# A cap of 768 KB on the transfers under way from SyncE's queue during the second pass

## The chip, the cores and the metric

The kernel runs on one core of one Trainium2 chip. The metric is the device time of one execution in microseconds. Before the change it is 1311.23 us, the median of three runs (1306.88 to 1315.88).

## The reference: what is computed

There are 32 batches (graphs) of 512 nodes with 128 features each, `x[32, 512, 128]`, and a symmetric 0/1 adjacency matrix with ones on its diagonal per batch, `adj[32, 512, 512]`, all in fp32. Four layers follow one another; each takes `h = relu(layernorm(x))` and adds its result to `x`:

```
layer 0  q, k, v = relu(h Wq' + bq), relu(h Wk' + bk), relu(h Wv' + bv)
         x += softmax_j(where(adj, q k', -9e15)) v
layer 1  dyn = conv3(h[:, last 128 nodes]);  lw = lstm(dyn)      # 128 steps, hidden size 128
         x += sigmoid((D^-1/2 (adj + I) D^-1/2 h) lw)
layer 2  four graph layers: tanh(cat(src_agg, own, dst_agg) Wu + bu),
         with adj normalised by rows and by columns; the 3rd and 4th also take earlier ones
x       += layer 2
layer 3  x += prelu(adj (h W'))
```

The LSTM runs over 128 time steps for all 32 batches at once. It needs the last 128 nodes of every batch after layer 0, and nothing of the other nodes. Everything from the sigmoid of layer 1 on needs `lw`, and so the end of the LSTM.

## The kernel before

`symmetric` records every operation in a planner (`Plan.op`) with the engines that may run it, an estimated duration, a rank, what it reads and writes, and a gap in which its result is on the way. `Plan.run` then simulates five engines with these estimates, gives every operation an engine and a start, sorts all of them by start, and emits them in that order. So each engine's queue, SyncE's (SP's) among them, is a fixed order of instructions; an instruction that waits holds back all that stands behind it on the same engine. A DMA is recorded by the helper `DMA` (line 853) with its size in KB; its place on SP's engine takes `0.1 + kb / 315` us in the plan, and its landing a gap of 2.0 us or, in the second pass, `LANDED = 3.8` us. Nothing of the plan's times is in the program; only the order is. What runs before what is kept by semaphores.

The work is in three passes over the batches and the LSTM.

- First pass, `pass_1` (ranks from 10,000): the layer norm, keys, values and the last 128 nodes of layer 0. Keys and hidden vectors (`f_dkq`), values (`f_dv`) and the last 128 rows (`f_dl`) go to HBM.
- The LSTM (`lstm`, ranks below 1,000 and 2,000 on): per step 16 small matmuls into `f_z` (L1224), two ScalarE tanh (L1250, L1262), VectorE (L1256, L1257), a tanh (L1264), VectorE (L1268, and L1269 for the transpose into `f_seq`), and then the next step.
- Second pass, `pass_2` (ranks 20,000 to 20,279 for batches 0 to 27; the last four batches have ranks above 30,000): layer 0 for the first 384 nodes. It is planned into the gaps of the LSTM. Per batch, SP's queue loads `f_h` (L1289) and `f_k` (L1290) from `f_dkq`, four blocks of the adjacency matrix of 256 KB each, `f_a` (L1293; L1298 with 192 KB for batches 22 to 25 and 28 to 31), the values `f_v` (L1300), `f_x` (L1301) and, for the batches that do the sums of layer 1 here, `f_dl` (L1304). ScalarE squares `f_a` into `f_ar` (L1363), TensorE makes the scores `f_s` (L1315), ScalarE their exponentials (L1318), VectorE multiplies with the mask (L1319), TensorE adds up `f_po` (L1324), VectorE updates `f_x` (L1328, L1330). For batches 0 to 21 the aggregation of layer 1, `f_pg` (L1409), follows. SP stores `f_dx` (L1335) and `f_dgT` (L1351). After four of the batches a `fold` of layer 2's weights is planned, with loads `f_rowb` (L986) and `f_w` (L988) of 384 to 768 KB.
- The rest, `rest` (L1423 on): for one batch after another all that needs `lw`, ended by the store to `out` (L1574). The first two turns (batches 26 and 27) have their ranks moved back by 9,950, so that they also lie between 20,000 and 30,000.

SP's queue carries 914 transfers; 88 of them are transposing transfers, which are recorded directly and not by `DMA`. The framework gives SP's DMAs eight semaphores in turn, and a DMA waits for the one eight before it, so that at most eight transfers are under way.

Of the kernel before, what the change touches and what calls it, by code (L numbers as in the profile page):

```python
# [492 lines left out]
class Cell:  # L493


    def __init__(self, pool, tag, shape, dtype, name, whole=False, filled=False):
        self.pool, self.tag, self.shape, self.dtype, self.name = pool, tag, shape, dtype, name
        self.whole, self.filled = whole, filled
        self.size = 1
        for n in (shape or ())[1:]:  # L500
            self.size *= n
        self.place = None
        self.ahead = 0
        self.marked = True
        self.real = None
        self.left = 0
        self.free_at = 0.0
        self.parts = {}
# [7 lines left out]


class Op:
    __slots__ = ("engines", "rank", "no", "deps", "cells", "waits", "ready", "end", "engine", "start", "next", "gap", "tiled", "patience")


class Plan:
# [22 lines left out]
    def __init__(self, bufs, fifo, banks):  # L545
        self.banks = banks
        self.last = float("inf")
        self.soon = 0.0
        self.spared = float("inf")
        self.left = 0  # L550
        self.sealed = 0
        self.kept = ("mm", "gs",)
        self.ops = []
        self.bufs = bufs
        self.made = {}
        self.fifo = {t: [] for t in fifo}
# [12 lines left out]
    def op(self, engines, rank, reads=(), writes=(), after=(), gap=0.0, tiled=False):  # L569

        o = Op()
        o.engines, o.rank, o.no, o.gap = engines, rank, len(self.ops), gap
        o.tiled = tiled
        o.patience = 0.15
        deps = set(after)
        cells = []
        for acc, is_write in [(a, False) for a in reads] + [(a, True) for a in writes]:
            c, part = acc if isinstance(acc, tuple) else (acc, None)
            if c not in cells:
                cells.append(c)  # L580
            for key, (ws, rs) in c.parts.items():
                if part is None or key is None or key == part:
                    deps.update(ws)
                    if is_write:
                        deps.update(rs)
            mine = c.parts.setdefault(part, ([], []))
            if is_write:
                c.parts[part] = ([o], [])
            else:
                mine[1].append(o)  # L590
        deps.discard(o)
        o.deps = list(deps)
        o.cells = [c for c in cells if c.pool is not None]
        for c in o.cells:
            c.left += 1
        self.ops.append(o)
        return o

    def run(self, tc, queues):
        import bisect  # L600
# [14 lines left out]
        for o in ops:  # L615
            if o.rank >= self.last:
                k, sub = divmod(o.rank - self.last, 10)
# [49 lines left out]
        def room(o):  # L667

            at = 0.0
            need = {}  # L670
            ahead = 0
            for c in o.cells:
                if c not in seen:
                    ahead = max(ahead, c.ahead)
                    if c.tag in self.fifo and self.fifo[c.tag][turn[c.tag] + need.get(c.tag, 0)] is not c:
                        return None
                    need[c.tag] = need.get(c.tag, 0) + 1
            for t, n in need.items():
                spare = n + ahead + (t == self.banks and o.rank >= self.spared and self.left > 0)
                if len(slots[t]) < spare or len(slots[t]) == spare and t in self.kept and by_rank and o.rank > by_rank[-1].rank + 12:  # L680
                    return None
                at = max(at, sorted(slots[t])[n - 1])
            return at
# [5 lines left out]
        tiled = False  # L689
        by_rank = sorted((o for o in ops if o.rank >= 10_000 and o not in apart), key=lambda o: -o.rank)  # L690
        while done < len(ops):
            best = None
            for e, cands in pools.items():
                first = None
                held = expected.get(e)
                for rank, no, o in cands:
                    r = room(o)
# [22 lines left out]
            s, e, o = best  # L720
# [6 lines left out]
            if e == "PE":  # L727
                tiled = o.tiled
# [22 lines left out]
            done += 1  # L751
        self.order = order
        order.sort(key=lambda o: (o.start, o.no))
        with tc.manual_schedule(engines=queues):
            for o in order:
                o.engines[o.engine][1]()


def symmetric(ctx, tc, x, adj, weights, cols, rows, lstm_b, prelu_a, out, fail):
# [26 lines left out]
    SOON = 9_950.0  # L786
# [18 lines left out]
    plan = Plan(BUFS, ("ar", "x", "inv", "n0", "n1", "n2", "n3", "a"), "mm")  # L805
# [32 lines left out]
    def t_dma(kb):  # L838
        return 0.1 + kb / 315.0
# [11 lines left out]
        return plan.op({"POOL": (t, fn)}, rank, r, w, **k)  # L851

    def DMA(rank, kb, fn, r=(), w=(), **k):
        return plan.op({"SP": (max(0.45, t_dma(kb)), fn)}, rank, r, w, gap=k.pop("gap", 2.0), **k)

    def turn_tiles(dst, src):

# [37 lines left out]
    w = const.tile([P, W_SD[0] + 1, P], FP, name="f_w")  # L895
# [16 lines left out]
    def load(rank, kb, dst, src):  # L912
        c = plan.fixed(dst)
        DMA(rank, kb, lambda: nc.sync.dma_start(dst, src), [], [c])
        return c

    w_att = load(HEAD + 0.1, 192, w[:, :W_CONV, :], weights[:, :W_CONV, :])
    w_cols = load(HEAD + 0.2, 5, colb, cols)
    DMA(HEAD + 0.3, 64, lambda: nc.sync.dma_start(brow[:, BR_V, :], rows[R_V].partition_broadcast(P)), [], [(biases, BR_V)])
    w_conv = load(HEAD + 12, 192, w[:, W_CONV:W_IH, :], weights[:, W_CONV:W_IH, :])  # L920
    w_crow = load(HEAD + 12, 64, conv_row, rows[R_CONV].partition_broadcast(P))
    w_lb = plan.fixed(lb)
    for j in range(P // TURN):
        part = bass.ts(j, TURN)
        DMA(HEAD + 100, 4, lambda part=part: nc.sync.dma_start(
            lb[part], lstm_b.rearrange("s q f -> (s q) f")[:, part].partition_broadcast(TURN)), [], [(w_lb, j)])
# [440 lines left out]
    def diagonal(rank, ar, op):  # L1367
        def fn():
            blocks = flat(ar.t).rearrange("p (k c) -> p k c", c=P)[:, :: NT + 1, :]
            nc.vector.tensor_tensor(blocks, f32(blocks), ident.unsqueeze(1).to_broadcast([P, NT, P]), op)  # L1370
        DVE(rank, t_dve(N), fn, [], [ar])
# [238 lines left out]
    end = lstm()  # L1610
# [5 lines left out]
        rest(b, k, end)  # L1616
    counted()
    E = mybir.EngineType
    plan.last, plan.spared, plan.soon = 30_000, 20_000, SOON
    plan.run(tc, {E.PE, E.Activation, E.DVE, E.Pool, E.SP})  # L1620
    return flag[0]

# [2 lines left out]
@with_exitstack  # L1625
def kernel(
    ctx: ExitStack,
    tc: tile.TileContext,
    x: bass.AP,
    adj: bass.AP,  # L1630
    weights: bass.AP,
    cols: bass.AP,
    rows: bass.AP,
    lstm_b: bass.AP,
    prelu_a: bass.AP,
    out: bass.AP,
):
    nc = tc.nc
    tensors = (x, adj, weights, cols, rows, lstm_b, prelu_a, out)
    flags = ctx.enter_context(tc.tile_pool(name="flags", bufs=1))  # L1640
    fail = flags.tile([P, 1], mybir.dt.int32, name="fail")
    with ExitStack() as pools:
        failed = symmetric(pools, tc, *tensors, fail)
    with tc.If(failed > 0, preferred_fallthrough_block=False), ExitStack() as pools:
        general(pools, tc, *tensors)
# [58 lines left out]
```

## Time and profile before

| | |
|---|---|
| median of three runs | 1311.23 us |
| the profiled execution's own time | 1314.59 us |
| its span in the profile | 1312.7 us |
| TensorE (PE) busy | 1272.8 us, 97% |
| VectorE busy | 988.7 us, 75% |
| ScalarE busy | 834.8 us, 64% |
| GpSimd busy | 393.3 us, 30% |
| DMA moved | 232.82 MB, mean 177 GB/s |
| granted TensorE clock | 0.994 |

The page has one profiled execution. A busy TensorE isn't TensorE at its peak, since matmuls are pipelined and their ends are modelled. The 40 slices of the page are 32.8 us each; the first pass fills slices 1 to 5 and, with the LSTM's first step at 184 us and its last at 500 us, the second pass fills slices 6 to 15. DMA digits are the mean busy share of the core's 16 DMA engines. A landing is the last update of a DMA's semaphore before the semaphore is used again.

### The profile page before, as it was taken

The numbers are of one execution on the slowest core, as the hardware profiler recorded it, in microseconds if no ns is written. First come the engines' busy times: TensorE is split into PE (matmuls) and PEld (weight loads), VectorE is DVE, ScalarE is ACT, GpSimd is POOL, SyncE is SP. The second block draws the span as 40 slices with busy tenths as digits, with TensorE's granted clock in tenths as the row PEclk, the third lists the DMA queues.
The fourth block names the chain that finished last, engine by engine and source line by source line (L and its number), as shares of the span: only waits on it lengthen the run. The fifth ranks groups of instructions, "written<-read, shape, count | busy, mean of one in ns | idle before, by whom it ended". The sixth has DMA issues, their size and how long they took to land.

```text
span 1312.7 us, 32944 instructions
## 1 busy us (share of the span) xinstructions
PE 1272.8 (97%) x12097; PEld 979.3 (75%) x12097; DVE 988.7 (75%) x3274; ACT 834.8 (64%) x2093; POOL 393.3 (30%) x733
## 2 busy tenths in 40 slices
PE   9999999999899999899999999999999999999996
PEld 6888866666567777677878778787787877877774
DVE  7999878778779887677667677676776787787654
ACT  5666667667678654577466666666666666675433
POOL 5655532112213233432213213132131332332000
PEclk9999999999899999999999999999999999999999
DMA  8888888847757867899377776777766465773311
GB/s 264 271 279 271 277 275 252 263 155 240 233 149 251 265 187 168 201 201 218 93 150 163 159 165 152 151 164 160 161 153 143 91 137 139 142 169 65 53 28 36
DMA packets 301259, 232.82 MB, mean 177 GB/s; under 512 B 139680, under 2 KB 246688, under 8 KB 301088
## 3 DMA queue, kind: packets, MB, share of 16 engines
q1 hardware_dynamic: 284192, 213.84, 59.4%
q0 software_dynamic: 16896, 16.78, 8.2%
q8 instruction: 98, 1.61, 0.5%
q14 instruction: 73, 0.60, 0.2%
HBM read 136.98 MB, written 62.13 MB: 152 GB/s over the span
## 4 chain that ended last, share of the span: by engine, by line
PE 85%; DVE 5%; ACT 3%; POOL 2%; DMA 2%; issue 2%; SPq 0%; ACTq 0%; DVEq 0%; POOLq 0%
PE f_pa L1409 17%; PE f_pa L1524 14%; PE f_py L1513 14%; PE f_pg L1409 9%; PE f_po L1324 5%; PE f_s L1315 5%; PE f_z L1224 4%; PE f_p L1565 2%; PE f_pol L1174 2%; PE f_pk L1131 2%; PE f_pv L1147 2%; PE f_pl L1467 2%; PE f_sl L1164 2%; PE f_pd L1199 1%; PE f_pq L1306 1%
## 5 line engine op out<-in xcount | busy, mean ns | idle before, releaser
L1409 PE MATMUL f_pa<-f_ar,f_y 128*128 128x512 f32 x1024 | 295.0, 426 | 2.1 <-ACT f_y L1392 2.1
L1409 PEld LDWEIGHTS f_pa<-f_ar,f_y 128*128 128x128 f32 x1024 | 189.3, 188 | 72.3 <-issue 35.8
L1513 PE MATMUL f_py<-f_wf,f_n 128*128 128x128 f32 x1280 | 173.5, 275 | 0.0
L1513 PEld LDWEIGHTS f_py<-f_wf,f_n 128*128 128x128 f32 x1280 | 164.4, 192 | 10.0 <-issue 1.9
L1524 PE MATMUL f_pa<-f_n,f_wf 128*128 128x512 f32 x320 | 152.9, 593 | 0.1
L1528 ACT ACTIVATE f_n<-f_pa,f_bcol 128x512 f32<-128x512 f32 x128 | 88.2, 689 | 93.6 <-PE f_pa L1524 93.4
L1363 ACT ACTIVATE f_ar<-f_a 128x512 fp32r<-128x512 f32 x216 | 133.7, 622 | 7.1 <-DMA f_a<-in_adj_dram 3.7
L1392 ACT CAST f_y<-f_py 128x512 fp32r<-128x512 f32 x128 | 74.8, 585 | 93.8 <-PE f_py L1513 90.7
L1481 POOL DMA_DIRECT2D f_das<-f_ar x32 | 27.9, 873 | 341.5 <-ACT f_ar L1363 267.9
L1324 PE MATMUL f_po<-f_v,f_e 128*32 128x129 f32 x3072 | 107.0, 274 | 7.5 <-issue 7.4
L1520 DVE TENSOR_TENSOR f_pa<-f_pa,f_inv 128x512 f32<-128x512 f32 x128 | 86.8, 694 | 27.7 <-PE f_pa L1409 27.4
L1324 PEld LDWEIGHTS f_po<-f_v,f_e 128*32 128x32 f32 x3072 | 90.4, 110 | 21.8 <-issue 15.2
L1393 DVE TENSOR_TENSOR f_y<-f_py,f_y 128x512 fp32r<-128x512 f32 x128 | 87.6, 685 | 24.1 <-ACT f_y L1392 23.8
L1315 PE MATMUL f_s<-f_q,f_k 128*32 128x384 f32 x1024 | 103.3, 490 | 0.6 <-issue 0.6
L1224 PE MATMUL f_z<-f_w,f_seq 128*32 128x128 f32 x2040 | 85.1, 277 | 8.6 <-DVE f_seq L1269 4.3
L1524 PEld LDWEIGHTS f_pa<-f_n,f_wf 128*128 128x128 f32 x320 | 57.5, 190 | 47.1 <-issue 37.8
L1224 PEld LDWEIGHTS f_z<-f_w,f_seq 128*32 128x32 f32 x2040 | 54.5, 109 | 45.1 <-ACT f_e L1318 8.7
L1486 DVE SCALAR_TENSOR_TENSOR f_junk<-f_a,f_aT 128x1024 bf16<-128x1024 f32 x64 | 78.1, 1220 | 5.7 <-DMA f_aT<-f_das 4.7
L1409 PE MATMUL f_pg<-f_ar,f_xp_d 128*128 128x512 f32 x256 | 75.2, 417 | 0.5 <-DVE f_lw L870 0.3
L1058 ACT ACTIVATE f_xn_c<-f_x,f_sh_c,f_rs_c 128x128 f32<-128x128 f32 x138 | 58.0, 486 | 24.2 <-DVE f_sh_c L1066 24.1
L1318 ACT ACTIVATE f_e<-f_s 128x384 f32<-128x384 f32 x128 | 60.7, 485 | 19.8 <-PE f_s L1315 14.8
L1513 PE MATMUL f_py<-f_wf,f_T_c 128*128 128x128 f32 x448 | 72.9, 275 | 0.0
(202 smaller groups left out, 2734.9 us busy)
## 6 DMA issues: line engine op xcount, KB each, us to landing
f_a<-in_adj_dram SPq DMA_DIRECT2D x30, 1024.0 KB
f_a<-in_adj_dram SPq DMA_DIRECT2D x96, 256.0 KB
f_das<-f_ar POOLq DMA_DIRECT2D x32, 512.0 KB, 4.8
f_dkq<-f_kh SPq DMA_DIRECT2D x32, 448.0 KB
f_dv<-f_v SPq DMA_DIRECT2D x32, 258.0 KB
f_v<-f_dv SPq DMA_DIRECT2D x32, 258.0 KB
f_x<-in_x_dram SPq DMA_DIRECT2D x32, 256.0 KB
f_al<-in_adj_dram SPq DMA_DIRECT2D x32, 256.0 KB
```

The lines of the kernel that those rows point to most:

```text
L1224: nc.tensor.matmul(z.t[part, k, :, :], h, w[:, m : m + 4, part], start=False, stop=True, skip_group_check=True)
L1315: PE(R, t_mm(NR), lambda s=s, j=j: quarters(lambda p: nc.tensor.matmul(s.t[p], keys.t[:, j * P + p.start : j * P + p.stop], q.t, start=Tru ...
L1324: PE(R, t_mm(P), lambda t=t, j=j: quarters(lambda p: nc.tensor.matmul(po.t[p, t, :], es[j].t[:, t * P + p.start : t * P + p.stop], v.t[:, ...
L1363: ACT(rank, 0.62, lambda t=t: nc.scalar.activation(ar.t[:, t, :], a.t[:, t, :], AF.Square, accum_out=deg.t[:, t : t + 1]), [(a, t)], [(ar, ...
L1392: ACT(rank, t_act(N), lambda: nc.scalar.copy(parts.t[:, :, 0, :], src.t), [src], [(parts, 0)])
L1393: DVE(rank, t_dve(N), lambda: nc.vector.tensor_sub(parts.t[:, :, 1, :], src.t, f32(parts.t[:, :, 0, :])), [src, (parts, 0)], [(parts, 1)])
L1409: nc.tensor.matmul(pg.t, parts.t[:, j, k, :], ar.t[:, j, :], start=(k == 0 and j == 0), stop=(k == 1 and j == NT - 1))
L1486: nc.vector.scalar_tensor_tensor(junk, flat(a.t[:, 2 * k : 2 * k + 2, :]), 1.0, flat(aT.t[:, 2 * k : 2 * k + 2, :]), OP.mult, OP.not_equal ...
L1513: nc.tensor.matmul(py.t[:, j, :], nodes[n].t[:, bass.ts(j, P)], wf[:, W_F[i] + c, 0, :], start=False, stop=(c == nch - 1), skip_group_chec ...
L1520: before = DVE(R, t_dve(N), lambda pa=pa: nc.vector.tensor_mul(pa.t, pa.t, inv_row.t), [inv_row], [pa])
L1524: nc.tensor.matmul(pa.t, wf[:, W_F[i] + c, 1, :], nodes[n].t, start=False, stop=(c == nch - 1), skip_group_check=True)
L1528: ACT(R, 0.57, lambda pa=pa, n=n, i=i: nc.scalar.activation(n.t, pa.t, AF.Tanh, bias=bcol[:, i : i + 1]), [pa], [n])
```

## The change

Every recorded transfer of SP's queue keeps its size in `kb` (0 for the transposing ones). While the instructions are emitted, a list `flight` of all SP transfers in order is kept. After each one `hold_back` is called. If the transfer's rank lies in 20,000 to 30,000 (the second pass of batches 0 to 27, its stores, the folds, and the first two turns of the rest), it goes back through the list, its own size first, until the sum is over 768 KB; on the transfer at which this happens it puts a dependence: this transfer is issued once that one has landed. Other transfers get no dependence, but count. The order of instructions on every engine stays as it was, since the plan doesn't look at `kb`.

```diff
+    def hold_back(self, tc, flight, o):
+
+        if not self.spared <= o.rank < self.last:
+            return
+        kb = 0
+        for ins, more in reversed(flight):
+            if kb + more > self.in_flight:
+                tc.add_manual_dep(flight[-1][0], ins.name, mybir.DependencyInfo(
+                    mybir.DependencyClass.Sync, mybir.DependencyReason.DATA), reason="transfers under way")
+                return
+            kb += more
...
+        flight = []
         with tc.manual_schedule(engines=queues):
             for o in order:
-                o.engines[o.engine][1]()
+                made = o.engines[o.engine][1]()
+                if o.engine == "SP":
+                    flight.append((made.ins, o.kb))
+                    self.hold_back(tc, flight, o)
...
     def DMA(rank, kb, fn, r=(), w=(), **k):
-        return plan.op({"SP": (max(0.45, t_dma(kb)), fn)}, rank, r, w, gap=k.pop("gap", 2.0), **k)
+        o = plan.op({"SP": (max(0.45, t_dma(kb)), fn)}, rank, r, w, gap=k.pop("gap", 2.0), **k)
+        o.kb = kb
+        return o
...
-    plan.last, plan.spared, plan.soon = 30_000, 20_000, SOON
+    plan.last, plan.spared, plan.soon, plan.in_flight = 30_000, 20_000, SOON, 768
```

More of the change, by code (lines that the diff above doesn't have):

```diff
@@ L518 @@
 class Op:
-    __slots__ = ("engines", "rank", "no", "deps", "cells", "waits", "ready", "end", "engine", "start", "next", "gap", "tiled", "patience")
+    __slots__ = ("engines", "rank", "no", "deps", "cells", "waits", "ready", "end", "engine", "start", "next", "gap", "tiled", "patience", "kb")
 class Plan:
@@ L548, in __init__ @@
         self.soon = 0.0
+        self.in_flight = float("inf")
         self.spared = float("inf")
@@ L574, in op @@
         o.patience = 0.15
+        o.kb = 0
         deps = set(after)
```

## The prediction

> **What bounds the kernel now.** I read the page's busy rows first, then the same rows of the second pass alone, then who waits there, then SP's own queue.
>
> ```profile
> span 1312.7 us, 32944 instructions
> PE 1272.8 (97%) x12097; PEld 979.3 (75%) x12097; DVE 988.7 (75%) x3274; ACT 834.8 (64%) x2093; POOL 393.3 (30%) x733
> DMA  8888888847757867899377776777766465773311
> GB/s 264 271 279 271 277 275 252 263 155 240 233 149 251 265 187 168 201 201 218 93 150 163 159 165 152 151 164 160 161 153 143 91 137 139 142 169 65 53 28 36
> ```
>
> TensorE is the busiest engine from end to end, but the change touches the part in which DMA is nearly full: in the first eight slices the rings are eight tenths busy and move 252 to 279 GB/s. The DMA answer for 160 to 480 us, the second pass beside the LSTM, in 40 slices of 8 us, shows what is asked of the queue there:
>
> ```profile
> GB/s 274 271 280 289 278 232 276 234 289 290 257 173 289 62 118 205 253 286 189 275 201 324 93 258 264 242 152 160 74 168 278 264 280 164 274 312 291 234 181 255
> DMA packets 54877, 74.30 MB, mean 232 GB/s; under 512 B 5261, under 2 KB 31469, under 8 KB 54809
> ```
>
> A mean of 232 GB/s made of bursts of 260 to 320 and troughs under 100. The waits of ScalarE in the same stretch show who sets the pace beside DMA:
>
> ```profile
> ACT f_th L1250 <- PE f_z L1224: 48.1, 76, 4.1
> ACT f_tcn L1264 <- DVE f_th L1257: 19.6, 40, 1.2
> ACT f_e L1318 <- PE f_s L1315: 11.3, 8, 4.9
> ```
>
> The LSTM's tanh waits for its own matmuls, 76 times. These stand in TensorE's queue among the matmuls of the second pass, so TensorE's order ties the two together: a second-pass matmul that waits for data holds the LSTM step behind it. No wait for `f_a` is in this list; the loads are in time, though not by much. SP's timeline shows how close the queue runs:
>
> ```profile
> 234.84 0.33 SPq L1335 DMA_DIRECT2D f_dx<-f_x  x1
> 235.21 0.43 SPq L1293 DMA_DIRECT2D f_a<-in_adj_dram  x1
> 235.74 0.39 SPq L1300 DMA_DIRECT2D f_v<-f_dv  x1
> 236.17 0.43 SPq L1301 DMA_DIRECT2D f_x<-in_x_dram  x1
> 236.65 0.49 SPq L1304 DMA_DIRECT2D f_x<-f_dl  x1
> 237.24 0.91 SPq L1289 DMA_DIRECT2D f_h<-f_dkq  x1
> 238.19 0.43 SPq L1290 DMA_DIRECT2D f_k<-f_dkq  x1
> 238.72 1.82 SPq L1293 DMA_DIRECT2D f_a<-in_adj_dram  x4
> 240.83 0.33 SPq L1300 DMA_DIRECT2D f_v<-f_dv  x1
> 241.20 0.43 SPq L1301 DMA_DIRECT2D f_x<-in_x_dram  x1
> 246.43 0.33 SPq L1335 DMA_DIRECT2D f_dx<-f_x  x1
> ```
>
> Thirteen transfers leave within 7 us, one each 0.5 us, far faster than they land: by the landing semaphores `f_a` of 239.61 lands at 245.67. The queue is filled ahead, and that depth keeps the rings busy while SP waits afterwards (241.6 to 246.4).
>
> **What the Trainium skill says.** "DMA: Bandwidth & Descriptors", Anatomy of one DMA, splits a transfer into a fixed part of about 2 us, mostly the write's receipt, and a part by bytes, and says that DMA engines never wait for semaphores: the issuing sequencer does. The trace agrees: with nothing else under way, `f_k` (256 KB) issued at 271.87 lands 2.82 us later, `f_v` at 376.60 after 2.60, and `f_dgT` at 278.27 after 2.51, though the rings pass a 256 KB transfer each 0.95 us at 275 GB/s. So several must be under way. Its table of latencies (Latency and other measured facts) has HBM answering more slowly at high load; the trace fits: with over 1 MB ahead of them `f_a` blocks need 4.5 to 6.2 us. This is the only way in which a smaller window gives something back.
>
> **The change, part by part.**
>
> *What it adds.* Counting sizes along SP's order by the rule of the diff, 324 of 914 transfers get a dependence, the 80th (issued at 70.3 us) to the 585th (597.8 us); 205 of them on the third transfer back, 76 on the fourth. A transfer and those that it leaves under way sum to 681 KB in the mean (697 kB in units of 1000). Against the trace's landings, 250 of the 324 were issued before the landing that they now wait for, 458 us if each is counted alone; so the waits bind. Under way were, in the mean of 20 us stretches, 800 to 1,160 KB where the rings were busy. The waiting itself costs SP an instruction word in some places, a row of 0.05 us or nothing: hidden in the wait.
>
> *What it removes and moves.* Nothing is removed, and the instruction order of each engine is the same. Everything behind the waiting transfer on SP waits too: at first the last loads of the first pass (160 to 190 us), then all loads and stores of the second. GpSimd's DMA queue has nothing in the second pass, so it gains nothing from emptier rings. The waits in 480 to 600 us (small `f_ddi`, `f_inv`, `out`) are late already by 2 to 6 us and cost nothing.
>
> *The price.* With the cap, 697 kB move per cycle of landing, release, issue, landing. A lone transfer needs 2.5 to 2.8 us from SP's instruction to landing; behind two others it needs more, since each takes 0.9 us of the rings. Lower bound of the cycle: 2.6 us, 268 GB/s. Upper: 3.4 us, 205 GB/s (with about 500 KB ahead the trace's 192 and 256 KB transfers needed 3.3 to 3.5 us after the issue). I take 3.1 us: 225 GB/s. In the 8 us slices above, 27 lie over 225, by 1,274 together: 1,274 x 8 / 225 = 45 us, if no trough is used to catch up. If all troughs are, 74.30 MB / 225 GB/s = 330 us against 320: 10 us. The middle is 28.
>
> *What of it lies on the path.* The troughs are mostly not free room: SP stands in them because it waits for compute (a store `f_dx` at 246.43 waits for VectorE; `f_k` at 267.56 for a buffer), and compute that is late moves them along. That speaks for the upper end. For the lower end speak the loads' lead: from landing to first use `f_v` has a median of 27 us and `f_k` over 50, but `f_a` only 4.0 to its square on ScalarE, with 22 of 88 under 3 us. About 4 us of lateness are swallowed once. Also TensorE's gaps, 18 of the 320 us (busy 302.0), are the LSTM's own latencies, and a wait for data overlaps some of them. Upper end less these, middle of the rest: I take +27 us. The chain is `f_a` late, square (L1363), mask (L1319), `f_po` (L1324), and `f_z` behind it in TensorE's queue; so the LSTM's last step moves from 500 to some 527 us.
>
> *Afterwards.* All that follows needs the LSTM's end (`gates`), is in the same order and has no new wait that binds: it moves as a block. Profiled execution: 1314.6 + 27 = 1341.6 around a span of 1339.7. The median of the runs is 3.4 lower, so I forecast 1311.2 + 27 = 1338.
>
> **The rivals.**
>
> *Hidden.* The window of three is enough: cycle 2.6 us, 268 GB/s. Slices over 268 are then cut by little (17 of them, 300 together: 300 x 8 / 268 = 9 us), and the lead of `f_a` covers 4 of these. Time 1311 to 1320. For it: the lone landings of 2.5 us, and emptier rings that answer faster. Against it: the smaller sizes make 681 KB, not 768, and two transfers ahead cost ring time.
>
> *The LSTM multiplies it.* The cycle is 3.4 us, 205 GB/s: the 27 slices over it give 1,814 x 8 / 205 = 71 us, and the 768 KB fold load at 346.0 (landing after 5.9) now travels alone. Time 1360 to 1385. For it: `f_a` needs over 4 us even today. Against: that is queueing which the cap removes.
>
> *Faster.* HBM at lower load serves better, and the shorter cycle overtakes the deep queue. The 27 busy slices run at 225 + 1,274 / 27 = 272 GB/s in the mean; at the 312 that one of them has, their 216 us of work would shrink by 28 us, and if compute used half of it, 1297 would come out. It decides from a cycle of 697 kB / 272 GB/s = 2.56 us, with three under way; only lone stores (2.0 us) and the lone loads of 2.5 us came that near. And compute gains only where it waits for these loads today, which the list of waits hardly shows. Unlikely.
>
> *It doesn't do what it says.* The framework's eight semaphores already cap transfers at eight, and the new dependences might be implied by these. In the built program they aren't: `f_a` at 175 us, which waited for one landing semaphore, waits for a later one or for two.
>
> **How the numbers follow.** Main case (1320 to 1358) 0.62; hidden 0.17; multiplied 0.16; faster 0.05. A measurement of this kernel can tell 1% (13 us) from no change. Faster by over 1%: 0.03; within 1% (to 1324), most of hidden, the rest of faster and the lowest part of the main case: 0.19; slower: 0.78. The range leaves out about 0.08 on either side: 1316 to 1372.
>
> **What would show it.** In the changed profile, GB/s of the second pass stay under 250 in the 8 us slices; SP's own waits name landings (`f_a`, `f_k`, `f_v`) for over 100 us together; the time from issue to landing falls to about 3 us; ScalarE's square waits for `f_a`; the first `f_th` without a successor, the LSTM's end, is at about 527 us, and the rest takes as long as before. I am wrong if the second pass keeps bursts of 275 and more, or if the LSTM ends late but the rest makes it good, or if the loss arises after 527 us.

## The result and the profile after

The changed kernel takes 1364.87 us (median of four runs, 1363.67 to 1367.21) against 1310.95 us for the kernel before (four runs, the three from above and one more): a ratio of 1.041 (95% interval 1.037 to 1.045), 54 us more. The forecast was 1338 us, 27 more, with a range to 1372. The direction held, and the cap binds as foreseen; the size was half of what came. The two profiled executions, 1314.59 and 1363.67 us, lie 49 us apart, and the readings of the traces below are of these two.

The page of the kernel after, the rows that answer to those of before:

```profile
span 1361.7 us, 32958 instructions
PE 1289.3 (95%) x12097; PEld 986.2 (72%) x12097; DVE 989.5 (73%) x3274; ACT 836.7 (61%) x2093; POOL 393.5 (29%) x733
DMA  8889876656765677898947777677776455664211
GB/s 257 267 276 279 257 210 205 207 165 190 212 191 159 195 212 217 187 204 223 182 88 167 150 163 159 159 157 168 150 152 163 111 116 133 150 145 101 47 32 34
```

The same work in a span 49.0 us longer. DVE, ACT and POOL are busy as long as before. TensorE isn't: for the same 12,097 matmuls it is busy 16.5 us longer (1289.3 against 1272.8) and idle 32.5 us longer. In slices 6 to 8, where the second pass begins, the rate is 205 to 210 GB/s instead of 252 to 275, and until the LSTM ends, in slice 17, it stays at 159 to 217. The DMA answer for 160 to 480 us, in slices of 8 us:

```profile
GB/s 253 144 228 217 192 241 202 193 187 192 247 217 226 174 196 217 181 85 151 215 160 207 206 220 235 178 196 185 178 226 195 219 143 94 139 226 192 207 204 180
DMA packets 44991, 62.01 MB, mean 194 GB/s; under 512 B 4371, under 2 KB 23685, under 8 KB 44933
```

The bursts of 270 to 320 are gone (the highest slice has 253); the same 320 us now move 62.0 MB instead of 74.3. What SP's queue waits for, in 160 to 560 us (lines are 20 higher than before: L1313 loads `f_a`, L1320 `f_v`, L1355 stores `f_dx`, L1371 `f_dgT`):

```profile
SPq L1313 <- DMA f_a<-in_adj_dram: 25.8, 37, 2.1
SPq L1320 <- DMA f_a<-in_adj_dram: 21.2, 13, 3.6
SPq L1371 <- DMA f_a<-in_adj_dram: 14.4, 12, 3.1
...
SPq L1313 <- DMA f_k<-f_dkq: 10.4, 11, 1.5
```

Landings now hold the queue. Summed over the second pass (160 to 550 us after, 160 to 500 before), such waits are 205 us; before they were 17. And the engines behind it wait, ScalarE first and then VectorE (waited for; us in total, times, longest), in 160 to 550 us:

```profile
ACT f_th L1270 <- PE f_z L1244: 48.0, 68, 2.6
ACT f_x L1078 <- DMA f_dx<-f_x: 31.9, 13, 6.2
ACT f_tcn L1284 <- DVE f_th L1277: 24.9, 46, 2.2
ACT f_ar L1383 <- DMA f_a<-in_adj_dram: 15.6, 18, 2.7
```

```profile
DVE f_x L1075 <- DMA f_dx<-f_x: 27.6, 12, 5.9
...
DVE f_e L1339 <- DMA f_a<-in_adj_dram: 8.2, 4, 5.3
```

The square (L1383) and the mask product (L1339) wait for `f_a`, as foreseen. The largest rows weren't: the layer norm that is written in place over `f_x` (L1075, L1078) waits until the store `f_dx` has read it. Before the change none of the computing engines but TensorE, once for 1.5 us, waited for a landing in this pass.

The LSTM's progress, step for step in the two traces, shows where the time went (start of `f_th` of that step, after less before):

| step | 0 | 16 | 32 | 48 | 56 | 64 | 80 | 96 | 112 | 127 |
|---|---|---|---|---|---|---|---|---|---|---|
| later by, us | 4.1 | 13.4 | 25.9 | 24.9 | 30.6 | 29.0 | 40.5 | 42.4 | 51.0 | 49.5 |

It rises where the bursts were (to step 32, around 80, around 100), is flat where DMA had troughs, and hardly falls. The last step starts at 549.7 us instead of 500.2. The rest is shifted as a block: 812.4 us from there to the end before, 811.9 after.

### The profile page after: what moved, and what is told of

Its sections match the earlier page's. It is cut to its first block, busy times and chain, and to the rows that moved or that the text cites. A ratio compares the mean times of both kernels' runs of the same rounds, so it can differ in the third digit from the quotient of the medians.

```text
span 1361.7 us, 32958 instructions
## 1 busy us (share of the span) xinstructions
PE 1289.3 (95%) x12097; PEld 986.2 (72%) x12097; DVE 989.5 (73%) x3274; ACT 836.7 (61%) x2093; POOL 393.5 (29%) x733
## 4 chain that ended last, share of the span: by engine, by line
PE 73%; DMA 15%; DVE 4%; ACT 3%; POOL 2%; issue 1%; SPq 1%; ACTq 0%; POOLq 0%; DVEq 0%
PE f_pa L1429 16%; PE f_py L1533 14%; PE f_pa L1544 14%; PE f_pg L1429 8%; DMA f_a<-in_adj_dram 6%; PE f_po L1344 3%; PE f_z L1244 2%; PE f_s L1335 2%; PE f_p L1585 2%; PE f_pk L1151 2%; PE f_pv L1167 2%; PE f_pl L1487 2%; PE f_pol L1194 2%; DMA f_h<-f_dkq 2%; PE f_sl L1184 2%; DMA f_v<-f_dv 2%
## 5 line engine op out<-in xcount | busy, mean ns | idle before, releaser
L1383 ACT ACTIVATE f_ar<-f_a 128x512 fp32r<-128x512 f32 x216 | 134.0, 623 | 23.6 <-DMA f_a<-in_adj_dram 19.7
L1078 ACT ACTIVATE f_xn_c<-f_x,f_sh_c,f_rs_c 128x128 f32<-128x128 f32 x138 | 58.0, 486 | 24.3 <-DVE f_sh_c L1086 24.3
L1429 PE MATMUL f_pg<-f_ar,f_xp_c 128*128 128x512 f32 x256 | 72.0, 424 | 0.1
```

What stands on the lines that cost most here:

```text
L1383: ACT(rank, 0.62, lambda t=t: nc.scalar.activation(ar.t[:, t, :], a.t[:, t, :], AF.Square, accum_out=deg.t[:, t : t + 1]), [(a, t)], [(ar, ...
L1429: nc.tensor.matmul(pg.t, parts.t[:, j, k, :], ar.t[:, j, :], start=(k == 0 and j == 0), stop=(k == 1 and j == NT - 1))
```

## The experiments

Three theories stood. A: the cap sets the rate of the loads, so many bytes per cycle of release, issue and landing. B: the dependences cost by their number, whatever the window. C, from the waits above: the late stores `f_dx`, which hold the norm in place, make the loss.

**Loads alone.** A kernel with nothing but loads of 256 KB, in seven groups of 32, each with a dependence on the load so many places back. It leaves out all four layers.

```diff
+WINDOWS = (1, 2, 3, 4, 5, 6, 8)
+COUNT = 32
...
+    for w in WINDOWS:
+        for k in range(COUNT):
+            b, t = divmod(k, 4)
+            i = nc.sync.dma_start(bufs[k], adj[b, t * P : (t + 1) * P, :])
+            made.append(i.ins)
+            back = w if k >= w else k + 1
+            if len(made) > back:
+                tc.add_manual_dep(made[-1], made[-1 - back].name, sync, reason="transfers under way")
```

> Transfers alone, with no computation: seven groups of 32 loads of 256 KB of adj, with at most 1, 2, 3, 4, 5, 6 and 8 under way; the layers are left out. Theory A (the cap sets the rate: so many bytes per cycle of release, issue and landing): about 3.1 us a load with one under way (85 GB/s), 165 GB/s with two, 205 to 230 with three, 265 with four, and no more from five on. Theory B (the dependences themselves cost, not the window): the rate grows to its top at two already, and all groups differ little. If HBM answers faster when less is under way, three reach 260.

The answer by stretch, one group each; the last number is GB/s:

```profile
0.73:82.29 81.56, 0.00 (x0) 0.00 (x0) 1.00 0.35 103
82.29:127.83 45.54, 0.00 (x0) 0.00 (x0) 1.00 0.62 184
127.83:162.65 34.82, 0.00 (x0) 0.00 (x0) 1.00 0.77 241
162.65:193.96 31.31, 0.00 (x0) 0.00 (x0) 1.00 0.83 268
193.96:222.42 28.46, 0.00 (x0) 0.00 (x0) 1.00 0.87 295
222.42:248.13 25.71, 0.00 (x0) 0.00 (x0) 1.00 0.91 326
248.13:272.79 24.66, 0.00 (x0) 0.00 (x0) 1.00 0.95 341
```

With 1, 2, 3, 4, 5, 6 and 8 loads of 256 KB under way the rate is 103, 184, 241, 268, 295, 326 and 341 GB/s. So the window sets the rate, beyond the five at which I expected it to level; B's picture of little difference falls. A's numbers were low for one to three (85, 165 and 205 to 230 were expected), and the 260 that faster answers of HBM would give three isn't reached. The mean time from the end of SP's instruction to landing grows from 2.19 us with one under way to 2.79 with three and 5.06 with eight, and from a landing to the end of the instruction that it releases it is 0.34 us with three. The fixed 2 us that the prediction takes from the Trainium skill ("DMA: Bandwidth & Descriptors", Anatomy of one DMA) stand there for transfers issued from GpSimd; on SP's queue, a lone load of 256 KB took these 2.19 us.

**Other caps.** The cap is a constant; 324 transfers get a dependence at each of the four values.

```diff
-    plan.last, plan.spared, plan.soon, plan.in_flight = 30_000, 20_000, SOON, 768
+    plan.last, plan.spared, plan.soon, plan.in_flight = 30_000, 20_000, SOON, 1024
```

(512 and 1536 likewise; with 512 a larger transfer waits for the one before it.)

> The cap at 512 KB, with the same 324 dependences. Theory A: 431 KB under way in the mean, 441 kB per cycle of 2.9 us, 152 GB/s; the 74.3 MB of the second pass need 490 us against 320: 1450 to 1500 us. Theory B (so much per dependence): as with 768 KB, 1365 us. Theory C (the stores f_dx that stand behind the cap hold the norm in place): the stalls grow with the delay of each store, about 1390.

> The cap at 1024 KB, with the same 324 dependences on older transfers. Theory A: 924 KB in the mean, 946 kB per cycle of 3.5 us, 270 GB/s, the rate that the bursts have without a cap: 1315 to 1328 us. Theory B: still 1365. Theory C: 1320 to 1335.

> The cap at 1536 KB, with the same 324 dependences, which are met at nearly every issue. Theory A and C: 1309 to 1315 us, as before the change. Theory B: 1365.

| cap, KB | time, us | ratio to before (95% interval) | last LSTM step later by, us |
|---|---|---|---|
| 512 | 1477.57 | 1.125 (1.123 to 1.127) | 156.5 |
| 768 | 1364.87 | 1.041 (1.037 to 1.045) | 49.5 |
| 1024 | 1332.06 | 1.014 (1.011 to 1.016) | 14.6 |
| 1536 | 1315.19 | 1.002 (1.000 to 1.004) | 0 (499.3 against 500.2) |

The same number of dependences costs 165 us or nothing, by the window: B is out, and a dependence that is already met has no price beyond the noise. The 1024 KB cap came out 4 us above the top of A's span.

**The stores.** Two kernels with `f_dx` on GpSimd's queue, with and without the cap, and two in which only the loads or only the stores have dependences.

```diff
-            DMA(R + 5, 192, lambda: nc.sync.dma_start(dx.t, xc.t[:, :L, :]), [(xc, t) for t in range(L)], [dx], gap=STORED)
+            DMA(R + 5, 192, lambda: nc.gpsimd.dma_start(dx.t, xc.t[:, :L, :]), [(xc, t) for t in range(L)], [dx], gap=STORED, store=True)
...
-                if o.engine == "SP":
+                if o.engine == "SP" and not o.store:
```

> The cap of 768 KB, but the 28 stores f_dx go out on GpSimd's queue, at the same place of the plan; they neither wait for a landing nor count. Theory A (late loads set the loss): the loads come as late as before, so 1345 to 1365 us, the waits for f_dx gone and those for f_a grown. Theory C (the store f_dx, held in SP's queue, holds the norm in place, 60 us of waits): 1320 to 1340.

> The same stores on GpSimd's queue and no cap: what the move itself costs or gives. Both theories: 1305 to 1318 us, no change; a gain of some us if SP's queue is short of time.

With the cap, 1360.31 us (ratio 1.038, 1.034 to 1.042); without it, 1313.48 (1.001, 0.999 to 1.003). The waits for `f_dx` are gone with the move, and in their place, in 160 to 560 us of the capped one:

```profile
ACT f_ar L1385 <- DMA f_a<-in_adj_dram: 30.1, 23, 5.2
DVE f_e L1341 <- DMA f_a<-in_adj_dram: 11.4, 3, 5.4
```

The waits for `f_a` have grown from 15.6 and 8.2 us to 30.1 and 11.4. The stores were the place where lateness showed first; the loads are its source. The move brings the last LSTM step 10 us forward (39.1 us late instead of 49.5), but the medians differ by 4.6 only, and the intervals of the two ratios overlap. In the profile of this kernel the rest takes 818.9 us after the LSTM's last step, instead of 811.9.

```diff
-        if not self.spared <= o.rank < self.last:
+        if o.store or not self.spared <= o.rank < self.last:
```

(`o.store` marks `f_dx` and `f_dgT`; the other kernel has `if not o.store or not ...` here.)

> The cap of 768 KB, with the dependences taken off the stores f_dx and f_dgT alone (some 49 of 324); they stay in SP's queue behind loads that wait. Theory A: 1350 to 1366 us. Theory C, if the stores' own dependences are what holds them: 1325 to 1340; if it is the loads ahead of them, 1350 to 1365.

> The reverse: only the stores f_dx and f_dgT have the dependence of 768 KB, the loads have none. A store may go when the third transfer or so ahead of it has landed, and what is behind it in the queue waits with it. Theory A: 49 waits, each shorter than 3 us, spread over the pass: 1315 to 1330 us. Theory C: over 1335.

With the stores free, 1367.13 us (1.044, 1.040 to 1.048): as with all held. With the stores alone held, 1313.87 (1.003, 1.002 to 1.005). So the stores' own dependences aren't the cause, and the kernel with `f_dx` off the queue showed that their place behind held loads isn't either: C is out in both forms. A's own 1315 to 1330 for the last was a little high: the waits of the stores alone are hidden.

**The mix alone.** SP's eleven transfers per batch of the second pass in their sizes, sources and order, eight batches under each cap, without any computation or layer.

```diff
+CAPS = (512, 768, 1024, 1536, 8192)
+BATCHES = 8
...
+        for cap in CAPS:
+            for b in range(BATCHES):
+                s = sets[b % 3]
+                go(192, cap, b == 0, s["h"], dkq[:, 512:])
+                go(192, cap, False, dx[b], keep[:, :384])
...
+                go(64, cap, False, s["l"], dl)
```

> SP's transfers of the second pass alone, with no computation: the eleven transfers of a batch in their sizes and row lengths (f_h, f_dx, f_k, four f_a, f_dgT, f_v, f_x, f_dl, 2434 KB together), eight batches under each of the caps 512, 768, 1024, 1536 KB and none but the framework's eight transfers. All layers are left out. If the mix itself makes the cycle of 3.4 us (smaller sizes, 512-byte rows of f_x, stores), 768 KB give 200 to 215 GB/s here too, 512 about 155, 1024 about 250, and none 300 or more. If the chain through compute (a load waits for a buffer, compute for the load) makes it, 768 KB give 230 to 250 here, as for equal loads alone (251).

By stretch, one cap each in that order; the last number is GB/s:

```profile
4.39:121.54 117.15, 0.00 (x0) 0.00 (x0) 1.00 0.55 171
121.54:211.58 90.04, 0.00 (x0) 0.00 (x0) 1.00 0.74 222
211.58:293.54 81.96, 0.00 (x0) 0.00 (x0) 1.00 0.81 243
293.54:358.63 65.09, 0.00 (x0) 0.00 (x0) 1.00 0.94 307
358.63:415.20 56.57, 0.43 (x1) 0.00 (x0) 1.00 1.00 353
```

768 KB give 222 GB/s: just outside both spans that I wrote down (200 to 215, 230 to 250), and 3 GB/s from the 225 of the prediction. The rings themselves could carry 353 GB/s of this mix with eight under way.

**Half of the pass.** The cap for batches 0 to 11 only, 144 dependences.

```diff
-        if not self.spared <= o.rank < self.last:
+        if not self.spared <= o.rank < self.spared + 120:
```

> The cap of 768 KB for ranks under 20,120 alone: batches 0 to 11 of the second pass and what has such ranks, 144 of the 324 dependences, the last of them at some 360 us. If late work isn't caught up in the troughs behind it, the LSTM ends as late as it was at that place with the full cap, 25 to 30 us: 1335 to 1343 us. If the troughs give it back: under 1325.

1335.83 us against 1310.04 beside it (ratio 1.021, 1.016 to 1.026). The LSTM is 24.4 us late at step 32, 26.2 at step 56 (350 us), 26.7 at 64, 25.8 at 96 and 24.5 at 127. After 350 us three transfers are still held, the last at 385 us; in the 140 us from there to the LSTM's end the queue has its full depth, and of some 26 us of lateness at most 2 are caught up.

## Why the prediction was half right

*The cap binds and the order stays.* Right: 205 us of SP's waits for landings (over 100 was foreseen), and from the end of SP's instruction to landing 2.85 us in the mean of the 324 instead of 3.61. The bursts stayed under 250 except for the first slice, 253.

*The price of the cycle.* Right: 2.85 us and the 0.34 us from a landing to the end of the released instruction make a cycle of 3.2 us, where 3.1 was taken; 225 GB/s was taken, the mix alone has 222.

*What of it lies on the path.* This step failed, in size: +27 us was taken, 49 came in the profiled execution and 54 in the median; the 5 between them lie within the spread of the runs before (1306.88 to 1315.88). It priced waits for data and let every matmul take as long as before. TensorE's busy time up to the LSTM's last step shows that this doesn't hold; first before, then after (busy PE, PEld, DVE, ACT, POOL; then the clock, DMA share, GB/s):

```profile
0.00:500.20 500.20, 478.35 (x7575) 360.59 (x7579) 413.15 (x1763) 336.42 (x1021) 177.36 (x406) 0.99 0.76 241
```

```profile
0.00:549.70 549.70, 493.75 (x7572) 366.02 (x7576) 414.31 (x1763) 337.99 (x1021) 177.63 (x405) 0.96 0.72 219
```

For the same matmuls (the edge of the stretch cuts three off) TensorE is busy 15.4 us longer and idle 34.1 us longer; together these are the 49.5 us by which the last step is late. So the waits for data cost 34 us instead of 27. The other 15 are a term that the prediction put at nothing: matmuls at half the granted clock, which come after such waits (last section).

Now the sum over the slices without any catching up can be held against both parts. With the rates of the mix it gives for 512 KB 132 us (2,826 x 8 / 171), for 768 KB 49 us (1,355 x 8 / 222), for 1024 KB 27 us (818 x 8 / 243) and for 1536 KB 0.6 us (22 x 8 / 307). For the half-capped kernel it is taken over the slices up to 320 and up to 360 us. The other columns are read like the two lines above, up to the LSTM's last step, as more than before:

| cap, KB | sum, us | last LSTM step, us | TensorE idle, us | TensorE busy, us |
|---|---|---|---|---|
| 512 | 132 | 156.5 | 115.6 | 40.9 |
| 768 | 49 | 49.5 | 34.1 | 15.4 |
| 1024 | 27 | 14.6 | 12.2 | 2.4 |
| 1536 | 0.6 | -0.9 | -1.1 | 0.2 |
| 768, batches 0 to 11 | 27 to 33 | 24.5 | 17.9 | 6.6 |

With 512, 768 and 1024 KB TensorE's idle time grows by 15 to 17 us less than the sum. The prediction took 18 off its 45 for the loads' lead and for gaps that TensorE had already; a discount of that size was about right. That the sum without a discount meets the whole lateness at 768 KB is luck, since the discount and the slower matmuls are equal there; with 512 KB it is 24 us short and with 1024 KB 12 too high. This is a reckoning from the traces, not an experiment: no run held the clock up, and without its fall TensorE might have waited longer instead. How much of the 15 us the fall really costs stays open.

*Why the troughs give nothing back.* The prediction said it itself: SP stands in them because it waits for compute, and compute that is late moves them along. In the step table the lateness is flat through the troughs and rises at each burst, and the half-capped kernel regains at most 2 us after its cap. It could hardly have regained more: before the change TensorE was busy for 125.5 of the 130 us from 370 to 500 us, whatever room DMA had there. Where the 15 to 17 us are swallowed, in the lead or in TensorE's earlier gaps, the runs don't show.

*The chain.* Incomplete. It named `f_a`, square, mask, `f_po`, `f_z`. That stores stand behind held loads was written down, but not who waits for them: the in-place norm of `f_x`, 59.5 us of waits on two engines. The runs with the stores moved or freed show that the omission cost little, since those waits only stand in for the ones for `f_a`.

*Afterwards.* Right: no recovery and no further loss after the LSTM's end; 49.5 us there, 49.0 at the end of the profiled execution.

*The rivals.* "Multiplied" came nearest in time (1360 to 1385) for the wrong reason: not a cycle of 3.4 us, but one of 3.2 with slower matmuls on top. "Hidden" is what a cap of 1536 KB does. "Faster" has nothing in its favour in any run: emptier rings do answer sooner (2.79 us with three against 5.06 with eight), but never so much sooner that the rate holds. The 4.5 to 6.2 us of blocks with over 1 MB ahead of them, which the prediction put beside HBM's slower answers at high load, don't show such a slowing: 1 MB alone takes the rings 3.8 us at 275 GB/s (an estimate).

## What to carry to other kernels

A cap on transfers under way is a cap on their rate, bytes under way over the time from release to landing; work that rate out and hold it against the bursts of the stage, not against its mean. Where the queue's troughs are waits for a busy engine, sum the excess over all slices and take off only what the loads' lead and that engine's idle time can swallow, here 15 to 17 us, not what the troughs would have room for. Then look at the busy time of that engine for the same work: here it grew by 15 us, which no list of waits shows. A wait placed on a queue also delays what merely stands behind it, stores included: ask which buffer each store frees.

## What was not expected of the hardware

- The rate of loads of 256 KB went on rising to eight under way (268 GB/s with four, 341 with eight), though most of the kernel's own bursts, at 250 to 290, looked like a ceiling.
- TensorE's granted clock fell in the second pass. The stretch of 160 to 480 us, first before, then after (busy PE, PEld, DVE, ACT, POOL; then the clock, DMA share, GB/s):

```profile
160.00:480.00 320.00, 302.03 (x5973) 215.21 (x5975) 254.05 (x1047) 221.50 (x775) 80.23 (x158) 0.99 0.74 232
```

```profile
160.00:480.00 320.00, 275.76 (x5075) 191.09 (x5073) 220.24 (x893) 197.20 (x682) 72.34 (x143) 0.95 0.65 194
```

Up to 550 us the trace has nine periods of 3.4 or 6.8 us at half the clock, 41 us together; before, two periods with 7 us. In the 3.4 us before each of the nine, TensorE stood idle for 1.7 to 3.4 us. One such wait, its period of half clock, and the time after it:

```profile
388.80:392.20 3.40, 0.00 (x0) 0.00 (x0) 1.61 (x5) 1.55 (x6) 0.00 (x0) 1.00 0.71 196
392.20:399.00 6.80, 5.52 (x104) 5.55 (x108) 4.43 (x15) 4.37 (x15) 0.48 (x2) 0.50 0.82 229
399.00:402.40 3.40, 3.40 (x96) 2.44 (x87) 3.03 (x18) 1.63 (x8) 1.67 (x4) 1.00 0.72 225
```

The idle time came from the cap: SP held the store `f_dx` until 388.7 us for the landing of `f_w` (768 KB), the norm on ScalarE (L1078) waited 6.2 us for that store, the LSTM's tanh stood behind the norm, and TensorE waited for the LSTM. In the half-clock period the LSTM's matmuls take 413 ns in the mean, against 275 from 440 to 480 us at full clock. "TensorE: Matmul & The Clock Gate" in the Trainium skill (Part 1: The HAM clock gate) describes such a halving after an idle window of about 3.4 us; the lengths of the periods agree, but TensorE wasn't always idle for the whole 3.4 us. So waits for data also make the work after them slower. Half of the 34 us more would be 17; TensorE's busy time up to the LSTM's end grew by 15.4.
